# Where the order is turned: transposes on DVE that write consecutively, and adds that read across

## The chip, the cores and the metric

The kernel runs on one core of one Trainium2 chip. Its time is the device time of one execution in microseconds (us). The time before is the median of three runs, 2492.71 us (2482.80 to 2496.35). Five engines work side by side: TensorE (PE) multiplies matrices, VectorE (DVE) and ScalarE (ACT) work element by element, GpSimd (POOL) issues some of the transfers and does small things, and SyncE (SP) issues the other transfers.

## The reference

The program is one transformer block, all in float32, on 2,048 tokens of 1,024 features. There are 32 heads of 32 features. The attention is over the heads of one token, not over tokens: for each token, 32 queries meet 32 keys.

```python
x = x + attn(layernorm(x), wq, bq, wk, bk, wv, bv)
x = x + ffn(layernorm(x), w1, w2, w3)

# attn, B = 1, S = 2048, H = 32 heads, D = 32
q = (h @ wq.T + bq).reshape(B, S, H, D)      # k and v alike
scores = einsum('bshd,bstd->bsht', q, k) / sqrt(D)
context = einsum('bsht,bstd->bshd', softmax(scores), v).reshape(B, S, E)

# ffn: each weight is first rounded to 16 levels (NF4) in blocks of 64
dq = NF4_CODE[searchsorted(bounds, w / absmax)] * absmax
h = silu(x @ dq1.T) * (x @ dq2.T)            # 2752 wide
out = h @ dq3.T
```

## The kernel before

The tokens are worked in 16 tiles of 128, two tiles to a pair, 8 pairs. Three sweeps over the pairs come first, each a loop `for p in range(NP)`: the query sweep (from the start to about 280 us), the key sweep (to about 545 us), the value sweep (to about 825 us). The feed-forward part follows and takes the rest.

In each sweep `products` computes one projection of a pair of tiles, 256 tokens by 1,024 features, with seven block products (Strassen's scheme) in place of eight. Its results are the two tiles `ce` and `co`, 128 tokens by 1,024 features each. For the attention the tokens of a pair have to change sides with features or heads, and this is done by DVE's transpose instruction, which turns blocks of 32 partitions by 32 elements:

- In the query sweep `qk_T` (lines 401 to 404) transposes `ce` and `co`, so that a partition holds one feature of a head, and adds the query bias. The result, 32 heads by 32 tokens per partition, goes to DRAM (`qD`) by a transfer on SP's queue.
- In the key sweep the same function makes the key tile `kd`, and the query tiles come back from DRAM as `ql`. `scores` (lines 413 to 425) multiplies them token by token: 64 products of 32x32 in each of the two parts of a tile. `softmax_T` follows on DVE and ACT, and its result goes to DRAM (`pD`).
- In the value sweep `v_T` (lines 406 to 411) makes the value tile `vd`, the probabilities come back as `pl`, and `context` (lines 427 to 440) multiplies them, again 64 products of 32x32 in each of two parts. `residual` (from line 649) transposes the contexts back out of PSUM into the tile `cx`, adds them to the tokens, stores the sum and normalizes it for the feed-forward part. `keep_T` then transposes the result on PE and stores it.

A matrix product of float32 shows as two records in the profile, so 64 products are 128 records.

What sets the order of the work: PE's instructions run in the order in which the program writes them. `products` calls `fill(n)` between its block products, and there a sweep puts pieces of other work: a part of the scores or of the contexts (`part()`), PE transposes, steps of the background. The background (`background`, `advance`) is the rounding of the weights to 16 levels; it runs all through the attention and most of the feed-forward part, almost wholly on DVE (lines 234 to 254) and ACT (lines 195 and 242), so many steps at each call. The instructions of the other engines are put in order by the framework's planner, which works from its own costs, and each engine works through its own queue in that order. Tiles come from pools: a pool's tag has a fixed number of buffers, and a new tile of that tag waits until the oldest buffer's last reader is done. `kd` and `vd` have three buffers, `qd` two, `cx` one.

The bias tiles hold one value per head feature: `qb_sb` and `kb_sb` are 32 features (on the partitions, four times over) by 32 heads, `vb_sb` 32 heads by 32 features likewise.

Of the kernel before, what the change touches and what calls it, by code (L numbers as in the profile page):

```python
# [12 lines left out]
FP = mybir.dt.float32  # L13
AF = mybir.ActivationFunctionType
ALU = mybir.AluOpType
# [3 lines left out]
P = 128  # L19
S = 2048  # L20
E = 1024
NH = 32
D = 32
# [46 lines left out]
def preln_block_kernel(  # L70
# [14 lines left out]
    nc = tc.nc  # L85
# [243 lines left out]
    def normed(src, dst):  # L329
        mv = small.tile([P, 2], FP, tag="mv", name="mv")  # L330
        rs = small.tile([P, 1], FP, tag="rs", name="rs")
        mean_var(small, src, mv)
        inv_std(rs, mv[:, 1:2])
        nc.vector.tensor_scalar(dst, src, mv[:, 0:1], rs, ALU.subtract, ALU.mult)
        return dst
# [58 lines left out]
    def differences(t, a21):  # L394
# [3 lines left out]
        nc.vector.tensor_tensor(t[:, S3], t[:, SA11], a21, ALU.subtract)  # L398
        nc.vector.tensor_tensor(t[:, S4], t[:, SA12], t[:, S2], ALU.subtract)

    def qk_T(t, c, b):

        nc.vector.transpose(t, c.rearrange("p (h d) -> p h d", d=D))
        nc.vector.tensor_tensor(t, t, b.unsqueeze(2).to_broadcast([P, 32, 32]), ALU.add)

    def v_T(t, c, b):

        nc.vector.transpose(
            t.rearrange("p m d -> p d m"), c.rearrange("p (t d) -> p d t", d=D)
        )  # L410
        nc.vector.tensor_tensor(t, t, b.unsqueeze(1).to_broadcast([P, 32, 32]), ALU.add)

    def scores(at, qd, kd, part):

        for s in range(16 * part, 16 * part + 16):
            c, s4 = s % 4, s // 4
            for g in range(4):
                r = slice(g * 32, (g + 1) * 32)
                nc.tensor.matmul(
                    at[c * 32 : (c + 1) * 32, g, s4 * 32 : (s4 + 1) * 32],  # L420
                    qd[r, :, s],
                    kd[r, :, s],
                    start=True,
                    stop=True,
                )
# [17 lines left out]
    work = sweep.enter_context(tc.tile_pool(name="workq", bufs=1, side="right"))  # L443
# [87 lines left out]
    for p in range(NP):  # L531
        more = p + 1 < NP
        now = nxt
        if more:
            load_x(2 * p + 2)
            load_x(2 * p + 3)
            nxt = Inputs(p + 1)

        def fill(n):
            if n in (7, 3):  # L540
                flush(1)
            if n == 5 and more:
                nxt.transposes(0)
                nxt.transposes(1)
            advance(0 if n == 5 else 1)

        cs = products(now.A, fill, (lambda name: None) if more else next_W("k"), ps_t)
        flush(1)
        if more:
            nxt.finished()  # L550
        for j in range(2):
            t = work.tile([P, 32, NH], FP, tag="qd", name="qd", bufs=2)
            qk_T(t, cs[j], qb_sb)
            nc.sync.dma_start(qD[2 * p + j], t)
        now.finished_v()
        weight_chunk("kv"[p // 4], p % 4)
        advance(2)
        if p == NP - 2:
            first = load_A(opD, 0)
# [4 lines left out]
    work = sweep.enter_context(  # L564
        tc.tile_pool(name="workk", bufs=1, side="right", reuse_waits="tile")
    )
# [26 lines left out]
    def attend(i, qd, kd):  # L593

        at = ps_at.tile([P, 4, 512], FP, tag="at", name="sc")
        scores(at, qd, kd, 0)
        yield
        scores(at, qd, kd, 1)
        nc.sync.dma_start(pD[i], softmax_T(at))
        yield  # L600
# [13 lines left out]
    def load_tiles(src, p, tag, bufs):  # L614
        ts_ = []
        for j in range(2):
            t = work.tile([P, 32, NH], FP, tag=tag, name=tag, bufs=bufs)
            nc.sync.dma_start(t, src[2 * p + j])
            ts_.append(t)
        return ts_  # L620

    A = first
    for p in range(NP):
        nextA = load_A(opD, p + 1) if p + 1 < NP else load_A(opV, 0)
        qd = load_tiles(qD, p, "ql", 3)

        def fill(n):
            if n in (7, 2, 5, 4):
                part()
            advance(1)  # L630
            if n in (3, 5):
                flush(1)

        cs = products(A, fill, (lambda name: None) if p + 1 < NP else next_W("v"))
        flush(1)
        for j in range(2):
            t = work.tile([P, 32, NH], FP, tag="kd", name="kd", bufs=3)
            qk_T(t, cs[j], kb_sb)
            parts.append(attend(2 * p + j, qd[j], t))
        advance(2)  # L640
        A = nextA
# [6 lines left out]

    def residual(i, at, x1):

        cx = work.tile([P, E], FP, tag="cx", name="cx")
        nc.vector.transpose(
            cx.rearrange("p (h d) -> p d h", d=D),
            at[:, :, 0:256].rearrange("p c (s d) -> p d s c", d=D),
        )
        nc.vector.tensor_tensor(x1, x1, cx, ALU.add)
        for n in range(2):
            nc.sync.dma_start(x1d[i][n], x1[:, ts(n, TB)])
        return normed(x1, x1)
# [16 lines left out]
    def gather(i, prT, vd):  # L676

        x1 = load_x1(i)
        at = ps_at.tile([P, 4, 512], FP, tag="at", name="cx")
        context(at, prT, vd, 0)  # L680
        yield
        context(at, prT, vd, 1)
        x1n[i] = residual(i, at, x1)
        yield
# [28 lines left out]
    for p in range(NP):  # L713
# [25 lines left out]
        if p == 0:  # L739
            sweep.close()  # L740
            sweep = ExitStack()
            work = sweep.enter_context(
                tc.tile_pool(name="workv", bufs=1, side="right", reuse_waits="tile")
            )
        pl = load_tiles(pD, p, "pl", 3)
        for j in range(2):
            t = work.tile([P, 32, D], FP, tag="vd", name="vd", bufs=3)
            v_T(t, cs[j], vb_sb)
            parts.append(gather(2 * p + j, pl[j], t))
# [399 lines left out]
```

## Time and profile before

| | us |
|---|---|
| median of three runs | 2492.71 |
| the profiled execution, whole | 2491.25 |
| its span, first to last instruction | 2489.5 |
| PE busy | 2385.8 (96%) |
| DVE busy | 1982.1 (80%) |
| ACT busy | 1610.2 (65%) |
| POOL busy | 279.8 (11%) |
| granted PE clock, mean | 0.987 of full speed |

The profile gives the busy time of each engine, and in windows the same for a stretch of the span. A group of instructions is one line of the program on one engine with its output, its inputs, its shapes and its count, then its busy time in us, the mean of one in ns, the idle time of the engine just before these instructions, and after the arrow what ended that idle time. A row of waits reads: engine and output that waited, what it waited for, us in all, how many times, the longest. "issue" is time in which the engine waited for nothing that the profile shows. L404 is line 404 of the program before.

### The profile page before, as it was taken

The numbers are of one execution on the slowest core, as the hardware profiler recorded it, in microseconds if no ns is written. First come the engines' busy times: TensorE is split into PE (matmuls) and PEld (weight loads), VectorE is DVE, ScalarE is ACT, GpSimd is POOL, SyncE is SP. The second block draws the span as 40 slices with busy tenths as digits, with TensorE's granted clock in tenths as the row PEclk, the third lists the DMA queues.
The fourth block names the chain that finished last, engine by engine and source line by source line (L and its number), as shares of the span: only waits on it lengthen the run. The fifth ranks groups of instructions, "written<-read, shape, count | busy, mean of one in ns | idle before, by whom it ended". The sixth has DMA issues, their size and how long they took to land.

```text
span 2489.5 us, 36718 instructions
## 1 busy us (share of the span) xinstructions
PE 2385.8 (96%) x14000; PEld 1119.6 (45%) x14000; DVE 1982.1 (80%) x2208; ACT 1610.2 (65%) x3267; POOL 279.8 (11%) x352
## 2 busy tenths in 40 slices
PE   7999999999899999999999999999999999899998
PEld 4444455545455444444444444444444444344433
DVE  7999788878988588989888899898988979871022
ACT  3556544444553378898888988889888888871200
POOL 1010000000000012030120301203012030120300
PEclk8999999999999999999999999999999999999999
DMA  8788643656669587394973939739496394872973
GB/s 309 280 315 327 239 161 116 231 210 218 215 226 324 195 292 166 110 199 148 327 163 119 199 145 323 170 110 207 154 293 174 128 198 157 283 152 72 198 268 138
DMA packets 177297, 513.90 MB, mean 206 GB/s; under 512 B 15904, under 2 KB 70176, under 8 KB 154720
## 3 DMA queue, kind: packets, MB, share of 16 engines
q1 hardware_dynamic: 136224, 438.08, 48.5%
q0 software_dynamic: 40320, 73.42, 18.2%
q8 instruction: 110, 1.80, 0.3%
q14 instruction: 67, 0.55, 0.1%
q10 hardware_dynamic: 576, 0.05, 0.0%
HBM read 283.69 MB, written 227.80 MB: 205 GB/s over the span
## 4 chain that ended last, share of the span: by engine, by line
DVE 18%; issue 17%; ACT 14%; PE 14%; DMA 4%; POOL 1%; DVEq 0%; SPq 0%; POOLq 0%; ACTq 0%
DVE r L243 11%; ACT sg L242 5%; PE z L339 5%; ACT wn L195 4%; PE z L976 4%; DMA x1d<-acc 3%; ACT acc L988 2%; ACT r L195 2%; PE y L976 2%; PE q L339 2%; PE r L976 1%; PE rr L339 1%; POOL x1d L990 1%; DMA out_dram<-acc 1%; ACT wop L162 1%
## 5 line engine op out<-in xcount | busy, mean ns | idle before, releaser
L243 DVE SCALAR_TENSOR_TENSOR r<-sg,r 128x1024 f32<-128x1024 f32 x780 | 945.8, 1214 | 98.1 <-ACT sg L242 66.8
L242 ACT ACTIVATE sg<-wn 128x1024 f32<-128x1024 f32 x780 | 812.4, 1053 | 307.0 <-DVE r L243 286.6
L990 POOL DMA_DIRECT2D x1d<-acc x280 | 244.5, 879 | 1285.7 <-ACT acc L988 1160.8
L339 PE MATMUL z<-xB,w 128*128 128x512 f32 x720 | 324.4, 600 | 5.2 <-ACT u L909 3.7
L339 PE MATMUL z<-xT,w 128*128 128x512 f32 x656 | 296.3, 594 | 5.4 <-ACT u L902 5.4
L339 PE MATMUL q<-xT,w 128*128 128x512 f32 x656 | 291.6, 592 | 0.0
L195 ACT ACTIVATE wn<-wn,rc 128x64 f32<-128x64 f32 x1032 | 267.4, 341 | 22.3 <-DVE rc L215 22.3
L976 PE MATMUL z<-w,h 128*128 128x512 f32 x496 | 236.8, 604 | 2.2 <-DMA w<-wd 1.7
L339 PEld LDWEIGHTS z<-xB,w 128*128 128x128 f32 x720 | 135.4, 192 | 172.4 <-issue 154.7
L339 PEld LDWEIGHTS z<-xT,w 128*128 128x128 f32 x656 | 121.7, 190 | 155.0 <-issue 136.9
L339 PEld LDWEIGHTS q<-xT,w 128*128 128x128 f32 x656 | 123.4, 190 | 149.4 <-issue 146.6
L339 PE MATMUL q<-wT,A 128*128 128x512 f32 x384 | 174.7, 598 | 3.0 <-DVE A L398 3.0
L339 PE MATMUL z<-wT,A 128*128 128x512 f32 x384 | 175.5, 600 | 1.8 <-ACT u L358 1.5
L976 PE MATMUL y<-w,h 128*128 128x512 f32 x320 | 153.9, 599 | 14.7 <-DVE h L963 12.7
L339 PE MATMUL z<-wB,A 128*128 128x512 f32 x320 | 153.0, 623 | 13.4 <-ACT u L358 13.2
L195 ACT ACTIVATE r<-r,am 128x64 f32<-128x64 f32 x608 | 155.1, 341 | 15.6 <-DVE r L243 15.2
L339 PE MATMUL rr<-xB,w 128*128 128x512 f32 x328 | 147.5, 592 | 0.0
L976 PEld LDWEIGHTS z<-w,h 128*128 128x128 f32 x496 | 93.7, 194 | 113.3 <-issue 98.1
L207 DVE TENSOR_REDUCE am<-wn 128x16 f32<-128x1024 f32 (+1 forms) x65 | 78.4, 1206 | 59.0 <-ACT r L195 53.2
L988 ACT COPY acc<-z 128x512 f32<-128x512 f32 x160 | 93.2, 582 | 35.7 <-PE z L976 31.7
L339 PEld LDWEIGHTS q<-wT,A 128*128 128x128 f32 x384 | 72.6, 192 | 91.1 <-issue 84.8
L339 PEld LDWEIGHTS z<-wT,A 128*128 128x128 f32 x384 | 70.4, 190 | 80.7 <-issue 77.1
(132 smaller groups left out, 2591.4 us busy)
## 6 DMA issues: line engine op xcount, KB each, us to landing
x1d<-acc POOLq DMA_DIRECT2D x280, 256.0 KB, 6.1
wd<-wop SPq DMA_DIRECT2D x31, 2048.0 KB, 7.2
w<-wd SPq DMA_DIRECT2D x41, 1280.0 KB, 7.6
wn<-in_w_dram SPq DMA_DIRECT2D x63, 512.0 KB, 4.7
xT<-xdT SPq DMA_DIRECT2D x28, 1024.0 KB, 8.0
xB<-xdB SPq DMA_DIRECT2D x24, 1024.0 KB, 6.1
w<-wd SPq DMA_DIRECT2D x42, 512.0 KB, 5.1
w<-wd SPq DMA_DIRECT2D x10, 1536.0 KB, 7.7
```

Source lines behind the costliest of these rows:

```text
L162: nc.scalar.copy(o[:q, first + half], pt[:q])
L195: nc.scalar.mul(dst[:, ts(n, BLOCK)], src[:, ts(n, BLOCK)], by[:, n : n + 1])
L207: nc.vector.tensor_reduce(am[:, :nb], v.rearrange("p (b e) -> p b e", e=BLOCK), AX.X, ALU.max, apply_absolute_value=True,)
L242: nc.scalar.activation(t, v, AF.Copy, bias=-edge * by, scale=by)
L243: nc.vector.scalar_tensor_tensor(r, t, code, r, ALU.min, ALU.max)
L339: nc.tensor.matmul(dst, w[:, k, :], xop[:, k, :], start=start and k == 0, stop=stop and k == 3, skip_group_check=True,)
L976: nc.tensor.matmul(dst, side[n][:, ts(q, P)], w3T[g[2 * m]][:, W3[n]], start=start and m == 0, stop=stop and m == 1, skip_group_check=True,)
L988: nc.scalar.copy(t, src)
L990: nc.gpsimd.dma_start(x1d[8 * tbp + 2 * q + j][n], t, accum_op=ALU.add)
```

## The change

A helper `turned` transposes into a scratch tile of 32 by 32 elements per partition, written consecutively, and returns a view of it with the two free dimensions exchanged. The bias add (queries, keys, values) or the add to the tokens (contexts) reads that view, with a step of 32 elements, and writes its result in the order wanted. Queries and keys, which were stored as heads by tokens, are now stored as tokens by heads, and `scores` takes its operands from there as 32 elements in a row. Values keep their layout; before, their transpose wrote it with a step of 32 elements. The same holds for the contexts. In the query and key sweeps the scratch tile is new (`turned`, one buffer, 4 KB per partition); in the value sweep it takes the buffer `cx` that the contexts had.

```diff
+    def turned(c, tag):
+
+        t = work.tile([P, 32, 32], FP, tag=tag, name="turned")
+        nc.vector.transpose(t, c)
+        return t.rearrange("p a b -> p b a")
+
     def qk_T(t, c, b):
 
-        nc.vector.transpose(t, c.rearrange("p (h d) -> p h d", d=D))
-        nc.vector.tensor_tensor(t, t, b.unsqueeze(2).to_broadcast([P, 32, 32]), ALU.add)
+        u = turned(c.rearrange("p (h d) -> p h d", d=D), "turned")
+        nc.vector.tensor_tensor(t, u, b.unsqueeze(1).to_broadcast([P, 32, 32]), ALU.add)
 
     def v_T(t, c, b):
 
-        nc.vector.transpose(
-            t.rearrange("p m d -> p d m"), c.rearrange("p (t d) -> p d t", d=D)
-        )
-        nc.vector.tensor_tensor(t, t, b.unsqueeze(1).to_broadcast([P, 32, 32]), ALU.add)
+        u = turned(c.rearrange("p (t d) -> p d t", d=D), "cx")
+        nc.vector.tensor_tensor(t, u, b.unsqueeze(1).to_broadcast([P, 32, 32]), ALU.add)
 
     def scores(at, qd, kd, part):
...
-                    qd[r, :, s],
-                    kd[r, :, s],
+                    qd[r, s, :],
+                    kd[r, s, :],
...
     def residual(i, at, x1):
 
-        cx = work.tile([P, E], FP, tag="cx", name="cx")
-        nc.vector.transpose(
-            cx.rearrange("p (h d) -> p d h", d=D),
-            at[:, :, 0:256].rearrange("p c (s d) -> p d s c", d=D),
-        )
-        nc.vector.tensor_tensor(x1, x1, cx, ALU.add)
+        cx = turned(at[:, :, 0:256].rearrange("p c (s d) -> p d s c", d=D), "cx")
+        xh = x1.rearrange("p (h d) -> p h d", d=D)
+        nc.vector.tensor_tensor(xh, xh, cx, ALU.add)
```

## The prediction

> **What bounds the kernel now.** I read the busy table first, then windows by stage, then the waits of each stage, then the groups of instructions that the change touches. The page's busy table says that TensorE (PE) works 96% of the span; the windows say where the remaining 4% lie. The five windows are the query sweep, the key sweep, the value sweep, the feed-forward part while DVE still dequantizes, and the rest. In each the columns are the width, then busy us of PE, weight loads, DVE, ACT and POOL, the granted clock, DMA share and GB/s.
>
> ```profile
> 20.00:280.00 260.00, 243.54 (x680) 114.11 (x681) 248.76 (x322) 155.32 (x338) 17.21 (x28) 0.97 0.83 310
> 280.00:545.00 265.00, 259.88 (x4583) 140.63 (x4574) 214.31 (x219) 112.24 (x217) 0.00 (x0) 1.00 0.46 169
> 545.00:825.00 280.00, 257.54 (x4679) 136.38 (x4678) 253.11 (x272) 132.25 (x275) 15.37 (x32) 0.96 0.73 244
> 825.00:2200.00 1375.00, 1337.87 (x3382) 603.31 (x3381) 1186.21 (x1286) 1143.79 (x2315) 216.23 (x248) 0.99 0.69 194
> 2200.00:2489.00 289.00, 275.31 (x672) 116.68 (x670) 72.13 (x101) 60.69 (x115) 28.45 (x33) 0.99 0.57 165
> ```
>
> The reader is to see three different stages. In the key sweep PE is idle for 265.0-259.9 = 5.1 us and DVE for 50.7 us: PE alone sets the pace. In the value sweep PE is idle for 22.5 us and DVE is at 90%. In the query sweep DVE is at 96% (98.7% between 100 and 200 us), yet PE too is close to full: an extra DVE microsecond there has little room, 11.2 us in all. After 825 us nothing that the change touches is left, and PE is at 97%, so time won or lost before 825 us moves the end one for one.
>
> The waits of PE in the value sweep, and then in the key sweep:
>
> ```profile
> PE z L339 <- ACT u L358: 12.6, 5, 4.3
> PE cx L433 <- issue: 6.1, 4, 2.7
> PE cx L433 <- DVE cx L652: 3.3, 1, 3.3
> ```
>
> ```profile
> PE sc L419 <- issue: 3.3, 2, 2.0
> PE sc L419 <- PE z L339: 1.7, 2, 1.0
> ```
>
> In the value sweep PE waits 12.6 us for ACT's copy of a product, which stands in ACT's queue behind activations that themselves wait for DVE (ACT `sg` of line 242 waits 79.9 us for DVE `r` there), and 3.3 us directly for the context transpose of line 652. In the key sweep DVE is in none of PE's waits.
>
> Now the instructions that change. First PE's two kinds of 32x32 products (columns: busy us, mean ns, idle before), then DVE's transposes and adds:
>
> ```profile
> L419 PE MATMUL sc<-kd,ql 32*32 32x32 f32 x4096 | 57.7, 262 | 5.1 <-issue 3.3 <-PE z L339 1.7
> L433 PE MATMUL cx<-vd,pl 32*32 32x32 f32 x4096 | 42.0, 200 | 9.5 <-issue 6.1 <-DVE cx L652 3.3
> ```
>
> ```profile
> L652 DVE STREAM_TRANSPOSE cx<-cx 128x1024 f32<-128x1024 f32 x16 | 31.4, 1962 | 1.1 <-PE cx L433 1.1
> L404 DVE TENSOR_TENSOR kd<-kd,kb 128x1024 f32<-128x1024 f32 x16 | 19.7, 1231 | 0.2
> L404 DVE TENSOR_TENSOR qd<-qd,qb 128x1024 f32<-128x1024 f32 x16 | 19.5, 1217 | 0.0
> L408 DVE STREAM_TRANSPOSE vd<-co 128x1024 f32<-128x1024 f32 x8 | 16.0, 1994 | 0.1
> L408 DVE STREAM_TRANSPOSE vd<-ce 128x1024 f32<-128x1024 f32 x8 | 15.9, 1984 | 0.5 <-ACT ce L383 0.5
> L403 DVE STREAM_TRANSPOSE kd<-ce 128x1024 f32<-128x1024 f32 x8 | 10.0, 1245 | 2.6 <-ACT ce L383 2.6
> ```
>
> Scores and contexts are the same number of products of the same size, and in both the row group of the array changes with every product; yet scores take 57.7 us and contexts 42.0. The difference in the code is that scores read both operands with a step of 32 floats (`qd[r, :, s]`) and contexts read 32 floats in a row. Among the transposes those that read and write in a row take 1.24 us (line 403), those that read and write with steps take 1.96 to 1.99 (lines 408 and 652).
>
> **The change, part by part.**
>
> *Scores read in a row.* After it, `qd[r, s, :]` and `kd[r, s, :]` are consecutive, the layout that contexts have. 57.7-42.0 = 15.7 us less PE time, all in the key sweep. The query tiles make a round trip through DRAM; they are whole tiles of 128x1024 in both versions, so no transfer changes in size or number. The part lies on the path that sets the end. Against it stands that DVE has to keep up with a sweep that is shorter: 214.3 us of DVE work in 249 instead of 265 us is 86% instead of 81%. Near 320, 420 and 480 us DVE is above 99% for 20 us at a time and PE waits 0.7 to 1.3 us there; I let that take 1.7 us back. Net -14.0.
>
> *Transposes of values and contexts write in a row, and still read with steps.* Price between 1.24 (line 403, no steps at all) and 1.99 us (line 408 as it is). The row that decides is line 652: it reads PSUM where line 408 reads SBUF, and writes SBUF with a step of 32 floats as line 408 does. Different sources, the same destination pattern, and 1.96 against 1.99: what they share is the writing. I therefore take 1.24 for both; 16 x (1.99-1.24) + 16 x (1.96-1.24) = 12.0+11.5 = 23.5 us less DVE work, in the value sweep alone. DVE goes from 253 to 230 us of 280, 82%, the share that it has in the key sweep, where PE is idle for 5 us instead of 22.5. I take half of that difference, -8 us, because the 12.6 us behind ACT also depend on ACT's bursts of sixteen small scalings. If the transposes stay at 1.99, this part is worth nothing.
>
> *Adds read with steps.* There are 16 each for queries, keys, values and contexts; each takes 1.21 to 1.23 us now. No two-input row of the trace reads with a step, so the price is bounded: from below by the present 1.22 (nothing about a step makes it cheaper); from above by the nearest row that moves 1,024 elements with steps on both sides, 1.99, +0.75 each. Here a rule of the Trainium skill speaks against the change: "SBUF — State Buffer", section "Door 1: The DMA port swizzle", says that an access pays a penalty whenever it moves on to another 16-byte line, and a step of 128 bytes does that with every element, reading as well as writing. Line 419 agrees for PE reads (57.7 against 42.0). Against it, "VectorE: DVE Perf Modes", section "Mode 1× (REGULAR) — the baseline", says that the mode of one element per cycle assumes nothing about steps and works with any, and 1,024 elements in 1.22 us, 512 in 0.69, are 1.04 ns per element, slow compared with PE's products. By the first rule at the trace's price the adds cost 64 x 0.75 = +48 us of DVE and the value transposes, still reading SBUF with steps, save nothing; by the second +0 and -23.5. PE's score products bear on it: one in four falls on a given row group, so every 57.7/4096 x 4 us = 56 ns each partition of that group reads 32 moving and 32 weight elements with steps, 0.88 ns each. That is less than DVE's 1.04. So I take +0.
>
> *Order and waits.* The transpose now goes into a scratch tile (`turned`, one buffer; for values the buffer `cx`, which the contexts use too). Writer and reader of the scratch are both on DVE, which works in order, so no engine waits for it. The wait for the older query store, or for the scores that read the older key tile, moves from transpose to add, one instruction later: nothing or a gain. Instruction counts are the same on all engines. PE's order is as before; the planner swaps a few neighbours on DVE (the second query transpose one statistic later, for instance) and on ACT, and on SP one query store goes behind one weight load. I take 0, with the 2 us of a pair's slack as its bound either way.
>
> *Sum*, against the profiled execution's own 2491.25 us (span 2489.5 and 1.75 around it): -14.0-8.0 = 2469.3. The median of the runs shown, 2492.7, is 1.5 above that execution, so 2470.
>
> **The rivals.**
>
> *Half price.* Adds +0.37, value transposes -0.37, context transposes (read from PSUM) -0.72. Query sweep +6 us of DVE, of which its idle 11.2 us absorb most: +3. Key sweep +6: 14.0 becomes -13. Value sweep 12-6-11.5 = -5.5 of DVE: -2. Sum -12: 2480. For it: PE's reads do get slower with steps.
>
> *Full price: DVE takes the place of PE as the bound.* Adds +0.75, values unchanged at 1.99. Query sweep: 1.5 us per pair of tiles, where DVE has 0.4 us free per pair in the middle of the sweep; 8 pairs, two of them with room, +7. Key sweep: DVE 226 of 249, 91%: 15.7 shrinks to 12. Value sweep: +24-11.5 = +12.5 of DVE, half seen by PE: +6. Sum +1: 2493. For it: the page's rule. Against it: line 652 equals line 408.
>
> *Slower.* One mechanism: reading SBUF with a step takes the two-input add to half rate. 1.04 ns more for each of 1,024 elements is +1.06 us per add, 2.28 in all. Query sweep +17 of DVE with 11 free: +11. Key sweep +17: DVE 93%, -8 left. Value sweep +34-11.5, +11. Sum +14: 2506. It decides from about +0.75 per add upwards. Against it: line 408 reads with a step as well and stays under 2.0 us.
>
> *The change doesn't do what it says*: scores stay at 57.7 us because their pace is not set by reading. Then only the -8 remain, 2484. Against it: lines 419 and 433 differ in nothing else that the profile shows.
>
> **How the numbers follow.** Likeliest case 0.55 (its own range 2459 to 2478); half price, with the change failing for scores, 0.20; full price 0.15; slower 0.10. The 80% range reaches down to 2456 (the value sweep gives the whole 17.5 us back instead of 8, and the key sweep the whole 15.7) and up to 2493, the full price. Less than 0.5%, 12.5 us, this kernel's measurement can't tell from no change, as its three runs lie between 2482.8 and 2496.4. Faster: nearly all of the first case and half of the second, 0.62; same: the other half and most of the third, 0.24; slower 0.14.
>
> **What would show it.** Scores near 42 us in their group and near 1.3 us per half; value and context transposes near 1.24; the adds after them still 1.22; the key sweep some 14 us shorter; PE idle in the value sweep nearer 14 than 22 us; the query sweep as long as before. Wrong if any of the four adds is above 1.4 us, if the value transposes stay near 2, or if a longer wait of PE for ACT or DVE eats the key sweep's gain.

## The result and the profile after

The changed kernel takes 2516.84 us (median of six runs, 2511.84 to 2520.34) against 2492.37 us of the kernel before: ratio 1.0101, 95% interval 1.0086 to 1.0116. It is slower by 24.5 us where 22 us less was forecast, and the time lies outside the range. The profiled execution took 2511.84 us, the fastest of the six, with a span of 2510.1 us; it shows 20.6 us of the loss.

The groups of DVE and of PE in the profile after (out<-in, count, busy us, mean ns of one, idle before). The transposes of all four kinds now stand on line 404. The first fence is the whole span, the second only 545 to 850 us, where line 404 holds the values' and contexts' transposes alone:

```profile
L657 DVE TENSOR_TENSOR x<-x,turned 128x1024 f32<-128x1024 f32 x16 | 31.3, 1953 | 0.2
L410 DVE TENSOR_TENSOR kd<-turned,kb 128x1024 f32<-128x1024 f32 x16 | 31.2, 1949 | 0.2
L415 DVE TENSOR_TENSOR vd<-turned,vb 128x1024 f32<-128x1024 f32 x16 | 31.1, 1942 | 0.0
L410 DVE TENSOR_TENSOR qd<-turned,qb 128x1024 f32<-128x1024 f32 x16 | 30.9, 1934 | 0.0
...
L437 PE MATMUL cx<-vd,pl 32*32 32x32 f32 x4096 | 42.3, 202 | 9.2 <-issue 4.8 <-DVE turned L404 4.4
L423 PE MATMUL sc<-kd,ql 32*32 32x32 f32 x4096 | 42.1, 203 | 14.8 <-issue 14.8
```

```profile
L404 DVE STREAM_TRANSPOSE turned<-cx 128x1024 f32<-128x1024 f32 x16 | 19.8, 1236 | 0.9 <-PE cx L437 0.8
L404 DVE STREAM_TRANSPOSE turned<-co 128x1024 f32<-128x1024 f32 x8 | 15.5, 1941 | 0.1
L404 DVE STREAM_TRANSPOSE turned<-ce 128x1024 f32<-128x1024 f32 x8 | 15.5, 1933 | 0.2 <-ACT ce L383 0.2
```

In these rows `turned` is the scratch tile, `ce` and `co` are the two tiles that a projection leaves, and `x` is the tokens.

All four adds went from about 1.22 us to between 1.93 and 1.95: their four means sum to 7.778 us after and 4.884 before, 16 x 2.894 = +46.3 us. The context transposes fell to 1.24, -11.6 us; the value transposes stayed (1.94 after 1.99), -0.8. That is +34; the busy table has DVE at 2014.6 us where it had 1982.1, +32.5. PE's scores fell from 57.7 to 42.1 us, as forecast, but the idle time before them rose from 5.1 to 14.8. Over the whole span PE is busy for 2380.5 us after 2385.8, 5.3 us less though the scores alone save 15.6, and idle for 25.9 us more: -5.3 and +25.9 are the 20.6 us of loss.

To see where the time went, I cut both spans at the first of the products that the profile calls `r` in each sweep (29.6, 256.7, 515.5 us before; 28.7, 262.5, 526.3 after) and at the first `rr` product of the feed-forward part (838.5 and 856.4). The four stages before, and then after; the columns are as in the windows of the prediction:

```profile
29.64:256.70 227.06, 213.43 (x586) 101.36 (x584) 219.02 (x295) 134.96 (x290) 17.21 (x28) 0.98 0.83 311
256.70:515.52 258.82, 251.59 (x4189) 134.18 (x4188) 214.28 (x217) 119.32 (x236) 0.00 (x0) 1.00 0.51 189
515.52:838.53 323.01, 300.15 (x5157) 157.99 (x5156) 277.41 (x300) 146.61 (x305) 15.59 (x32) 0.97 0.69 231
838.53:2489.47 1650.94, 1600.05 (x4017) 713.92 (x4015) 1254.16 (x1380) 1202.81 (x2426) 244.47 (x280) 0.99 0.67 188
```

```profile
28.67:262.53 233.86, 214.44 (x586) 101.29 (x585) 227.43 (x292) 133.96 (x289) 16.84 (x28) 0.97 0.78 295
262.53:526.31 263.78, 243.42 (x4190) 122.16 (x4189) 227.26 (x221) 119.35 (x236) 0.00 (x0) 0.97 0.51 191
526.31:856.42 330.11, 301.52 (x5157) 157.28 (x5156) 288.99 (x298) 146.57 (x305) 15.94 (x32) 0.96 0.67 225
856.42:2510.07 1653.65, 1601.35 (x4017) 713.08 (x4015) 1253.68 (x1380) 1205.47 (x2426) 245.08 (x280) 0.99 0.67 188
```

-1.0 before the first cut, +6.8 in the query sweep, +5.0 in the key sweep, +7.1 in the value sweep with its passage to the feed-forward part, +2.7 after it: 20.6. The key sweep is the surprise. Its scores take 14.1 us less (38.3 after 52.3; the rest of the scores lies behind the cut), but PE's busy time fell by only 8.2 us, and its idle time rose from 7.2 to 20.4. The missing 5.9 us of busy time go with the granted clock, 0.97 after 1.00.

This is one execution, and the split between the sweeps is not the same in every one. The run with a step of 33 floats (below), which has the same instructions and nearly the same time (2519.2 us), shows +9.3 in the query sweep, -0.3 in the key sweep and +11.3 in the value sweep. In both the saving of the scores is gone.

### The profile page after: what moved, and what is told of

It is laid out like the page before. It is cut to its first block, busy times and chain, and to the rows that moved or that the text cites. A ratio compares the mean times of both kernels' runs of the same rounds, so it can differ in the third digit from the quotient of the medians.

```text
span 2510.1 us, 36720 instructions
## 1 busy us (share of the span) xinstructions
PE 2380.5 (95%) x14000; PEld 1105.6 (44%) x14000; DVE 2014.6 (80%) x2208; ACT 1611.8 (64%) x3267; POOL 280.4 (11%) x352
## 4 chain that ended last, share of the span: by engine, by line
issue 29%; PE 13%; ACT 10%; DVE 10%; DMA 5%; POOL 1%; SPq 0%; DVEq 0%; POOLq 0%; ACTq 0%
DVE r L243 6%; PE z L339 4%; DMA x1d<-acc 4%; ACT sg L242 3%; ACT wn L195 3%; PE z L977 2%; ACT acc L989 2%; PE q L339 2%; ACT r L195 1%; POOL x1d L991 1%; PE y L977 1%; PE po L1045 1%; PE rr L339 1%; PE po L1056 1%; PE r L977 1%
## 5 line engine op out<-in xcount | busy, mean ns | idle before, releaser
L989 ACT COPY acc<-z 128x512 f32<-128x512 f32 x160 | 93.6, 585 | 32.5 <-PE z L977 27.7
```

The costliest lines, as they stand in the source:

```text
L989: nc.scalar.copy(t, src)
```

## The experiments

Times are medians. The kernel before ran beside them at 2490.5 to 2494.8 us, on more than one chip, so the ratios are the better measure.

**The scores alone, unpaid.** Only PE's reading changes, out of the old layout; each product mixes heads and tokens.

```diff
-                    qd[r, :, s],
-                    kd[r, :, s],
+                    qd[r, s, :],
+                    kd[r, s, :],
```

> The kernel before, with one edit: the scores read 32 floats in a row out of the old layout (heads by tokens), so each product mixes heads and tokens and the numbers are not the reference's; DVE does exactly what it did. It shows what the 15.7 us of PE time are worth when nothing is paid for them. Theory A (the key sweep is paced by PE, and the loss of the changed kernel is the price of DVE's adds alone): about 14 us less than before, near 2478. Theory B (the key sweep is paced by DVE, which frees the score banks late, so PE only waits longer): at most 4 us less, 2488 to 2492, with the waits of PE for the score banks some 10 us longer.

2484.85 us, ratio 0.9972 (0.9963 to 0.9982): 6.6 us less, between the theories. The scores took 41.8 us, so 15.9 us of PE time were saved, and more than half of that did not reach the end. In the profile of this run (an execution of 2492.8 us) the scores of the key sweep take 14.4 us less, the sweep is 3.9 us shorter: PE's idle time rose by 5.6 us, and 4.9 us of busy time are missing at a granted clock of 0.97.

**The adds alone, unrewarded.** The changed kernel, with scores reading with steps.

```diff
-                    qd[r, s, :],
-                    kd[r, s, :],
+                    qd[r, :, s],
+                    kd[r, :, s],
```

> The changed kernel, with the scores reading with steps of 32 floats again (out of the new layout, so that heads and tokens are mixed and the numbers are not the reference's): DVE pays for the adds, PE does not get the faster scores. Theory A (PE paces the key sweep): 14 us more than the changed kernel, near 2531. Theory B (DVE paces it): at most 4 us more, 2517 to 2521.

2523.04 us, ratio 1.0126 (1.0098 to 1.0153): 31.6 us more than before and 6.2 more than the changed kernel, though with four executions the intervals of the two overlap. With the run above this makes a table of two by two that adds up: DVE's 32 to 35 us cost 31.6 us (24 to 38 by the interval), PE's 15.7 us bring 6.2 to 6.6, and 31.6-6.6 = 25.0 stands against 24.5 measured. DVE's time comes through almost one for one, though it is busy for only 80% of the span. It does not come through as waiting alone: in the profile of this run PE is idle for 22 us more than before and busy for 11 us more (2396.8 after 2385.8), with no more to do.

**A step that is no power of two.**

```diff
-        t = work.tile([P, 32, 32], FP, tag=tag, name="turned")
+        t = work.tile([P, 32, 33], FP, tag=tag, name="turned")[:, :, 0:32]
```

> The changed kernel with the rows of the scratch tile 33 floats apart instead of 32: the adds read with a step of 132 bytes, no power of two. Theory 'banks' (a step of 128 bytes keeps hitting the same part of the memory): the adds fall from 1.94 us towards 1.22, DVE loses 46 us of work and the time falls to about 2470. Theory 'lines' (any step that leaves the line costs): the adds stay at 1.94 us and the time at about 2517.

2519.22 us, ratio 1.0100 (1.0073 to 1.0127), as the changed kernel; the adds took 2.00 to 2.01 us. It is not the power of two.

**The price by itself.** A prologue on 1,024 floats per partition, three times each; the name says the side (`rd` reads, `wr` writes with the step, `rdwr` both) and the step (`rdpadded`: 33 floats). In short, not word for word, with `across(t, s)` for `t` read or written with a step of `s` floats:

```python
nc.vector.tensor_tensor(o, across(flat, s), two, ALU.add)    # rd, s = 1, 2, 4, 8, 16, 32
nc.vector.tensor_tensor(across(q, s), flat, two, ALU.add)    # wr
nc.vector.transpose(across(o, 32), across(flat, 32))         # tboth; tread, twrite, tnone alike
nc.scalar.copy(o, across(flat, 32))                          # aread; awrite, anone alike
```

> The kernel before with a prologue of isolated instructions on 1024 floats per partition: DVE adds that read one operand, or write, with a step of 1, 2, 4, 8, 16, 32 and 33 floats, adds that read and write with a step of 32, transposes that read, write or do both with a step of 32, and ScalarE copies with a step of 32 on either side. Only these rows count, not the time (some 70 us of prologue). 'Lines': nothing up to 2 or 4 floats (8 or 16 bytes), then a jump to about 1.95 us for reading and writing alike, step 33 like 32, and both sides together no dearer than one. 'Banks': dearer with every doubling of the step, and step 33 cheap.

Groups of the prologue on DVE, some left out, and then on ACT (mean ns after the comma):

```profile
L125 DVE TENSOR_TENSOR rdone<-src,two 128x1024 f32<-128x1024 f32 x3 | 3.7, 1226 | 0.0
L125 DVE TENSOR_TENSOR rdtwo<-src,two 128x1024 f32<-128x1024 f32 x3 | 3.7, 1238 | 0.0
L125 DVE TENSOR_TENSOR rdfour<-src,two 128x1024 f32<-128x1024 f32 x3 | 5.9, 1976 | 0.0
L125 DVE TENSOR_TENSOR rdthirtytwo<-src,two 128x1024 f32<-128x1024 f32 x3 | 5.7, 1895 | 0.0
L137 DVE TENSOR_TENSOR rdpadded<-src,two 128x1024 f32<-128x1024 f32 x3 | 6.0, 1990 | 0.0
L130 DVE TENSOR_TENSOR wrtwo<-src,two 128x1024 f32<-128x1024 f32 x3 | 3.7, 1237 | 0.0
L130 DVE TENSOR_TENSOR wrfour<-src,two 128x1024 f32<-128x1024 f32 x3 | 6.0, 1987 | 0.0
L141 DVE TENSOR_TENSOR rdwr<-src,two 128x1024 f32<-128x1024 f32 x3 | 6.0, 1997 | 0.0
...
L149 DVE STREAM_TRANSPOSE tnone<-src 128x1024 f32<-128x1024 f32 x3 | 3.7, 1225 | 2.0 <-POOL src L113 2.0
L149 DVE STREAM_TRANSPOSE tread<-src 128x1024 f32<-128x1024 f32 x3 | 5.8, 1945 | 0.0
L149 DVE STREAM_TRANSPOSE twrite<-src 128x1024 f32<-128x1024 f32 x3 | 5.7, 1898 | 0.0
L149 DVE STREAM_TRANSPOSE tboth<-src 128x1024 f32<-128x1024 f32 x3 | 5.9, 1971 | 0.0
...
L155 ACT COPY awrite<-src 128x1024 f32<-128x1024 f32 x3 | 6.2, 2058 | 0.1
L155 ACT COPY aread<-src 128x1024 f32<-128x1024 f32 x3 | 6.1, 2023 | 0.0
L155 ACT COPY anone<-src 128x1024 f32<-128x1024 f32 x3 | 3.2, 1066 | 0.0
```

A step of 2 floats (8 bytes) is free, one of 4 (16 bytes) costs the full 0.75 us, and a longer one no more (1.88 to 2.01 us for 8 to 33). Reading and writing cost the same, and both together cost it once. ScalarE pays as well: 1.07 us without a step, 2.02 reading and 2.06 writing with it.

**Queries, keys and scores alone.** `v_T` and `residual` as before.

> Only queries, keys and scores changed; values and contexts as before. DVE has 16 x 0.72 us more in the query sweep and as much more in the key sweep, and what it had in the value sweep. From the traces of both kernels the value sweep of the changed kernel is some 7 us longer, so near 2507 if that is the values' adds (16 x 0.7 us); near 2517 if the value sweep is longer for another reason, such as coming out of the key sweep with more work queued.

2507.49 us, ratio 1.0062 (1.0043 to 1.0081): 16 us of the 25 are theirs, the other 10 or so (1.0101-1.0062 of 2492, some 6 us either way) belong to values and contexts, where DVE has 11 us more. The first reading holds: the value sweep of this run is 1.8 us longer than before, that of the changed kernel 7.1.

**The contexts alone.** `residual` of the changed kernel in the kernel before.

> The kernel before with the contexts' part of the change alone. The transpose writes in a row (1.24 instead of 1.96), the add reads across (1.95 instead of 1.21): DVE's sum stays, the context bank is free 0.7 us earlier and the tokens' sum is ready at the same time. Theory C: no change, 2490 to 2493. Rival D: up to 3 us less.

2494.37 us, ratio 1.0003 (0.9995 to 1.0012): no change. The price moved from the transpose to the add. That the bank was free 0.7 us earlier was worth nothing.

**No crossing in SBUF for the contexts.** PE's operands are exchanged, so that a token's context comes out with the features on the partitions and the heads in a row.

```diff
-                        prT[r, m, :],
                         vd[r, m, :],
+                        prT[r, m, :],
...
-            cx.rearrange("p (h d) -> p d h", d=D),
-            at[:, :, 0:256].rearrange("p c (s d) -> p d s c", d=D),
+            cx.rearrange("p (h d) -> p h d", d=D),
+            at[:, :, 0:256].rearrange("p c (s h) -> p h s c", h=NH),
```

> The kernel before with the two operands of the context products exchanged, so that a context comes out of PE with features on the partitions and heads in a row; its transpose then reads PSUM with steps, writes in a row, and the add after it reads in a row: nothing crosses SBUF. Theory C (from the runs so far: DVE paces the three sweeps, and its time comes through nearly one for one): transposes 1.24 instead of 1.96 us, 16 x 0.72 = 11.5 us less DVE in the value sweep, 8 to 11 us less than before, near 2482. Rival D (only PE's waits on late score and context banks count, not DVE's load): the bank is free 0.7 us earlier per tile, a part of the 3.3 us of waits goes, 2489.

2485.28 us, ratio 0.9978 (0.9970 to 0.9986): 5.5 us less by the ratio, faster than both kernels. The groups of its transposes and adds:

```profile
L652 DVE STREAM_TRANSPOSE cx<-cx 128x1024 f32<-128x1024 f32 x16 | 19.9, 1241 | 2.6 <-PE cx L433 2.6
L656 DVE TENSOR_TENSOR x<-x,cx 128x1024 f32<-128x1024 f32 x16 | 19.5, 1219 | 0.2
```

Both rows are at their price without a step, though the transpose reads PSUM with one: in this transpose the step costs nothing. The 11.5 us of DVE brought half of what theory C named at best.

**Less background in the key sweep.**

```diff
-            advance(1)
+            advance(0 if n == 6 else 1)
```

> The kernel before with one background step fewer per pair in the key sweep (after the product named 6): 8 steps of 1.22 us on DVE, about 10 us, move out of the key sweep to later. Theory C: the key sweep is shorter by 6 to 10 us, though its scores are still read with steps; the whole by as much, unless the feed-forward part then waits for weights. Rival D: DVE is 81% busy there, the steps only fill its gaps, the key sweep stays within 2 us.

2504.27 us, ratio 1.0050 (1.0034 to 1.0065). The key sweep took 258.1 us after 258.8: the 6 to 10 us of theory C did not come, which looks like rival D. But PE is idle for only 7.2 us in that sweep of the kernel before, so little could be won there and the run can't tell the two apart. The value sweep was longer and the feed-forward part waited for weights, 14.4 us in two waits.

**ScalarE does the turn.** This is an edit of the run with exchanged operands. The copy is shown; the scores read in a row as in the changed kernel.

```diff
+        nc.vector.transpose(u, c.rearrange("p (h d) -> p h d", d=D))
+        nc.vector.tensor_tensor(u, u, b.unsqueeze(2).to_broadcast([P, 32, 32]), ALU.add)
+        nc.scalar.copy(t, u.rearrange("p a b -> p b a"))
```

> The first kernel of this set, and ScalarE does the turn of queries and keys: DVE transposes and adds in a row as before (1.24 and 1.22), then a ScalarE copy of 2.0 us reads across and writes tokens by heads, and the scores read in a row. Theory C: DVE's load stays at the first kernel's, PE saves 15.7 us, of which the run with free scores showed 6.6; 32 copies of 2.0 us on ScalarE, 55% and 42% busy in these sweeps: 3 to 6 us less than the first kernel. Rival: ScalarE's copies stand ahead of the products' copies that PE waits for, and the gain is gone or reversed.

2502.94 us, ratio 1.0045 (1.0029 to 1.0061), slower by 18 us than without the turn: the gain is reversed, as the rival said, but not where it said. The copies took 2.0 us and the key sweep 274 us, at a granted clock of 0.94. PE's waits for ACT's product copies are only 3.9 us there; 15.1 us stand in front of the scores, of which 10.8 end when DVE has read the score bank. Why these waits are longer than the 6.7 us of the first experiment stays open.

**The scores' parts spread.** One product lies between the last scores of a tile and the first of the next, which need the only score bank. In both kernels, and in the first experiment, waits of PE end within 0.11 us after DVE has read that bank: one of 1.3 us in the key sweep before, three of 3.2, 4.6 and 3.7 us after, three of 1.3, 3.1 and 2.3 us in the first experiment. The profile puts them down to "issue". At the same place in the sixth pair, DVE's and PE's rows of the timeline before and after (start, duration, then idle time before):

```profile
423.16 1.23 DVE L577 TENSOR_TENSOR pr<-sc,mx 128x1024 f32<-128x1024 f32 x1
...
424.49 1.28 PE L419 MATMUL sc<-kd,ql 32*32 32x32 f32 x87 [1.27 <-issue]
```

```profile
429.98 1.22 DVE L581 TENSOR_TENSOR pr<-sc,mx 128x1024 f32<-128x1024 f32 x1
...
431.29 0.95 PE L423 MATMUL sc<-kd,ql 32*32 32x32 f32 x61 [4.57 <-issue]
```

(The first experiment has 3.08 us here.) Spreading the parts gives DVE two products' time:

```diff
-            if n in (7, 2, 5, 4):
+            if n in (7, 6, 5, 3):
                 part()
```

> The changed kernel with one more edit: in the key sweep the four parts of the scores stand after the products 7, 6, 5 and 3 instead of 7, 2, 5 and 4, so that two products and not one lie between the last scores of a tile and the first of the next, which have to wait until DVE has read the single score bank. Theory E (PE's saving in the key sweep went into waits for that bank, 14.8 against 3.3 us, and into the half clock that follows the long ones, 17 us of it): the waits of the scores fall below 4 us, no half clock in the sweep, the key sweep 12 us or more shorter, the whole near 2504. Rival F (DVE's load as a whole paces the sweep): the wait only moves to another place, under 4 us less than the changed kernel.

2508.30 us, ratio 1.0058 (1.0040 to 1.0076): less than the changed kernel by 8.5 us by the medians and 10.7 by the ratios, between E and F. The longest waits of PE in its key sweep:

```profile
PE z L339 <- ACT u L358: 9.2, 5, 3.5
PE sc L423 <- issue: 4.3, 3, 2.0
PE q L339 <- DVE co L390: 2.7, 1, 2.7
```

The waits in front of the scores went from 14.8 to 4.3 us, and none of those left ends with a read of the bank; they stand in the middle of a part, and nothing in the profile ends them. Waits for ACT and DVE in front of other products rose from 5.6 to 11.9 us. The half clock, which E expected to vanish, stays: 13.7 us of this sweep after 17.1. In this profile (an execution of 2513.4 us) the sweep is 262.2 us long after 263.8, so it does not show where the 8.5 to 10.7 us were won. My reading is that the bank is where DVE's lateness was paid, not what makes it late.

**The same spread without and with the turn of queries and keys.** Two runs, both with exchanged context operands.

> The kernel before with exchanged context operands (2485.3 in the earlier run) and the scores' parts spread as in the run before this one; scores still read with steps. The key sweep of the kernel before has 7 us of idle PE and no half clock, so theory E gives 1 to 4 us less than 2485.3; rival F the same time.

2483.91 us, ratio 0.9959 (0.9944 to 0.9975): 1.4 us less than without the spread by the medians, 4.7 by the ratios, but the two intervals overlap, so E and F stay undecided here. It has the lowest time of this study.

> The same with the queries', keys' and scores' part of the change (DVE's adds read across, 16 x 0.72 us each in the query and the key sweep; PE's scores read in a row). Theory E: the key sweep some 10 us shorter than in the kernel without, the query sweep 7 us longer: 2 to 5 us less than that one, near 2479. Rival F: as the runs before, 16 us more than without, near 2500.

2495.94 us, ratio 1.0019 (1.0010 to 1.0028). No wait of PE for the bank is left here either, yet queries, keys and scores of the change still cost 0.6% (1.0019 after 0.9959), as they do in the kernel before (1.0062). That is near rival F and far from E's 2479.

## Why the prediction was wrong

*The scores' price* was right: 42.1 us against 42.0 forecast.

*The price of reading across* is the first step that failed. I took +0 for the adds and 1.24 us for the value transposes; they measured +0.72 and 1.94, so DVE got 32 to 34 us more to do instead of 23.5 less. The inference from line 652 was half right: both transposes paid for writing. But line 408 would have paid the same for reading, and paid only once for both, which two rows of equal length can't show. Splitting it into a transpose that reads across and an add that reads across paid twice. The other inference, from PE's 0.88 ns per element, compared a different engine. The rule about 16-byte lines in the Trainium skill, "SBUF — State Buffer" (section "Door 1: The DMA port swizzle"), was the right one to take; the prologue has its jump between 8 and 16 bytes. Where the same passage lets float32 stride for free over 4 elements, the measurement decides: a step of 4 floats cost the full price, 1.98 against 1.23 us. The passage that I set against it says that steps work, not what they cost.

*The key sweep's pace* is the second. I put -14.0 on that sweep: the scores' saving, less 1.7 us for DVE. Its scores did save 14.1 us; 13.1 us more of waiting and 5.9 us at the lower clock took it back, and the sweep came out at +5.0. The full-price rival had DVE's price right to a few hundredths of a microsecond and still came out at 2493, with -12 for the key sweep. The step "PE alone sets the pace" rested on an average of 81% DVE and on DVE standing in none of PE's waits. But one wait that the profile puts down to "issue", 1.3 us long, ended with DVE's read of the score bank, and the average does not hold pair by pair. The second to the eighth pair of the key sweep, cut at their first `r` product, before; then five of them after:

```profile
285.00:317.60 32.60, 32.60 (x577) 17.84 (x576) 25.04 (x27) 12.56 (x28) 0.00 (x0) 1.00 0.44 171
317.60:350.10 32.50, 31.75 (x570) 16.99 (x569) 31.87 (x31) 17.07 (x30) 0.00 (x0) 1.00 0.38 140
350.10:382.20 32.10, 32.10 (x574) 17.40 (x573) 21.57 (x22) 11.13 (x29) 0.00 (x0) 1.00 0.38 141
382.20:414.30 32.10, 32.10 (x574) 17.40 (x573) 26.25 (x27) 10.78 (x13) 0.00 (x0) 1.00 0.29 108
414.30:447.60 33.30, 31.95 (x570) 17.09 (x569) 29.66 (x31) 19.78 (x46) 0.00 (x0) 1.00 0.43 152
447.60:480.10 32.50, 32.50 (x577) 17.80 (x576) 25.62 (x28) 9.38 (x13) 0.00 (x0) 1.00 0.48 176
480.10:515.50 35.40, 32.39 (x573) 17.51 (x572) 32.51 (x32) 18.36 (x33) 0.00 (x0) 1.00 0.89 329
```

```profile
293.00:323.50 30.50, 30.50 (x577) 15.74 (x576) 24.46 (x27) 11.73 (x27) 0.00 (x0) 1.00 0.43 165
323.50:356.40 32.90, 29.75 (x569) 14.99 (x568) 32.73 (x32) 14.68 (x19) 0.00 (x0) 1.00 0.42 155
...
418.30:454.70 36.40, 31.83 (x570) 15.91 (x569) 33.93 (x33) 19.98 (x47) 0.00 (x0) 0.91 0.35 125
454.70:485.20 30.50, 30.50 (x577) 15.74 (x576) 24.52 (x26) 8.23 (x13) 0.00 (x0) 1.00 0.53 195
485.20:526.30 41.10, 34.44 (x573) 17.42 (x572) 36.38 (x35) 19.44 (x34) 0.00 (x0) 0.88 0.77 293
```

In a pair where DVE has 25 us to do, PE has the 2.0 us (32.5 to 30.5). In the pair from 317.6 us DVE already had 31.87 of 32.5 us to do; the pair stays 32.9 us long, and PE's 2 us become waiting, 3.2 us after 0.8. In the two longest pairs the waits grew and the clock was halved for a part of the time as well. The prediction named these places, "near 320, 420 and 480 us", and put 1.7 us on them. These are the same three pairs in the run with unpaid scores, where DVE had nothing extra to do:

```profile
314.80:345.90 31.10, 29.79 (x569) 14.99 (x568) 30.89 (x31) 15.51 (x24) 0.00 (x0) 1.00 0.40 147
406.10:441.50 35.40, 32.32 (x569) 16.12 (x568) 30.95 (x32) 19.65 (x46) 0.00 (x0) 0.90 0.38 137
472.10:510.60 38.50, 32.88 (x573) 16.64 (x572) 33.38 (x34) 18.30 (x33) 0.00 (x0) 0.91 0.84 314
```

They were 1.4 us shorter and 2.1 and 3.1 us longer than before, while the other four were 1.3 to 2.0 us shorter.

*The query sweep* (full price +7, measured +6.8) and *the value sweep* (+6, measured +7.1) look well sized by that rival, but the closeness is in part the luck of this execution: in the four other runs with this query sweep whose adds have the step of 32 floats it is 9.4 to 10.2 us longer than before, and in the three other runs with these values and contexts (one with the step of 33) the value sweep is 8.9 to 11.3 us longer. *Order and waits* at nothing held as far as it shows: no wait for the scratch tile is seen, and PE's waits for the context transpose are 4.4 us after 3.3. One sum of the prediction is off: the lower end of its range, 2456, is not what its terms give, 2492.7-15.7-17.5 = 2459.5. Nothing hangs on it.

What stays open is whether DVE's time in the value sweep weighs the same both ways: 11.5 us bring 5.5 when they are taken away (3.5 to 7.5 by the interval), and values and contexts cost about 10, some 6 either way, when as much is added. The two ranges overlap.

## What to carry to other kernels

Look for the one pass that has to cross anyway, and let it cross on both sides: here a step of 16 bytes or more in SBUF made DVE's adds and transposes of 1,024 float32 some 60% longer, once, whichever side it was on, so a crossing split over two instructions was paid twice, while the transpose of the contexts out of PSUM crossed for nothing. Do not read from a stage's average which engine sets its pace: cut it at its own period, and count a saving only in those periods in which the other engine has room for it.

## What the runs showed of the hardware

A wait of PE can cost more than its length. The wait of 4.57 us in the sixth pair of the key sweep, which ended at 431.29 us, shows this (windows before, during and after; PE's clock is the third column from the right):

```profile
422.60:429.50 6.90, 4.12 (x66) 1.81 (x52) 6.69 (x7) 4.23 (x4) 0.00 (x0) 1.00 0.44 156
429.50:436.40 6.90, 5.11 (x132) 3.00 (x133) 6.87 (x8) 4.61 (x9) 0.00 (x0) 0.51 0.28 78
436.40:443.20 6.80, 6.80 (x142) 3.55 (x141) 5.77 (x5) 4.32 (x14) 0.00 (x0) 1.00 0.36 111
```

The clock record has the half clock in pieces of 3.4 and 6.8 us: none in the key sweep before, 17.1 us after, 13.7 in the run with unpaid scores. At most half of that, 8.5 and 6.8 us, is lost on top of the waits, since a piece can begin in a wait, as here at 429.5 us; PE's busy time shows 5.9 and 4.9. The length of a wait alone does not decide. In the changed kernel a wait of 3.0 us had a half clock at its end and those of 3.2 and 3.5 us had none; with the parts spread, waits of 2.0 us had one within 1.4 us after them, while in the kernel before waits of 2.0 and 2.1 us had none. The Trainium skill, "TensorE: Matmul & The Clock Gate", section "Part 1: The HAM clock gate (the "warmup" mystery)", describes a free-running window of about 3.4 us, which fits the pieces' lengths and would let the place of a wait in the window matter; no run here tests it.

Over the whole span the six executions of the changed kernel were granted 0.979 to 0.983 of the clock, the 91 of the kernel before that were timed beside the experiments 0.983 to 0.991, with means of 0.981 and 0.987. By an estimate from these figures (the span times what is missing to 1) that is 49 us against 32 us. Part of the 17 us falls in waits, where it costs nothing, but it is large beside the 24.5 us of the loss. With the scores' parts spread the mean is 0.985. So much of DVE's delay may have reached the end by way of the clock; no run separates the two.

The two engines' prices differ little: DVE 1.23 to 1.9 or 2.0 us, ScalarE 1.07 to 2.02 or 2.06. And PE's 32x32 products in float32 took 0.26 us a record with a step of 32 floats on both operands and 0.20 without; over 4,096 records, which overlap, that is 57.7 against 42.1 us.
